# A two-layer graph network on one core: node products moved in layer 0's drain, and mixes one chunk further ahead in layer 1's tables

## The chip, the cores and the metric

The kernel runs on one core of a Trainium2 chip (trn2). Its time is device time in microseconds (us). The core's engines are TensorE (PE in the profile; PEld is its weight loading), VectorE (DVE), ScalarE (ACT), GpSimd (POOL) and SyncE (SP, which issues most of the transfers). Each engine takes its own queue of instructions, and engines wait for each other through semaphores.

## What is computed

The reference runs two message-passing layers on a graph of 6250 nodes with 128 features and 106250 edges, sorted by destination (100000 random ones and a loop at each node). Cut to what matters:

```python
h = relu(layernorm(x))
# layer 0: attention (GATv2) with a residual, gelu, batch norm over nodes
m = leaky_relu(xl[src] + xr[dst] + edge_attr @ We, 0.2)      # xl = h @ Wl + bl, xr = h @ Wr + br
logits = m @ att
alpha = softmax of logits over the edges of one dst
h0 = gelu(h + segment_sum(xl[src] * alpha, dst) + bias_out)
x = x + ((h0 - mean) * rsqrt(var + eps) * bn_gamma + bn_beta) # mean, var over all nodes
# layer 1: messages, gate and update
h = relu(layernorm(x))
em = relu(layernorm(concat(h[src], h[dst]) @ msg_w + msg_b)) * edge_weight
messages = segment_mean(em, dst)
h_new = relu(layernorm(concat(h, messages) @ upd_w + upd_b))
x = x + gate * h_new + (1 - gate) * h                         # gate = sigmoid(h @ gate_w + gate_b)
```

## The kernel before, in words

The program holds two arms and a flag that the data decide; the sorted input takes the arm `fast()`, and only it is spoken of here. `fast()` works under a manual schedule: on each engine the instructions stand in the order in which the Python code issues them, and waits come from the data.

The edges are cut into NS = 99 blocks of up to 8 tiles of 128 edges (the last has 5 tiles). The loops of a node's own go into the per-node steps. The nodes are 49 tiles of 128, in NGR = 13 groups (`GS`): eleven of 4 tiles (groups 0 to 10), one of 3 (group 11) and one of 2 (group 12).

**Layer 0** is a loop over rounds `s` (line 1407), 0 to 106. Round s gathers block s from the table xl_d (POOL, L187), expands the destination rows by one-hot matmuls (L1132) and makes the logits. Every SB = 4 blocks a generator `maxima` takes the segment maxima over the tiles of four blocks (the last one of three): a transpose on PE (L1181), scans on DVE (L1184 to L1189), transposes of the ends (L1192, L1193), a row of carries on DVE (`crow`, L1196 to L1204), its transposes (L1208), a second scan (L1211 to L1215), an exp on ACT (L1216), and transposes back (L1219, L1220) to the factors `exm` (L1224). LAG = 7 rounds later, block u = s - 7 is weighted by these factors (`glw`: L1439 and L1444 on DVE, L1446 on ACT), summed by 8 one-hot matmuls in `agg_ps` (L1483, of two passes each in the profile), copied by ACT (L1321, in `flush` one round later) and stored to one of two tables by block parity (L1135, SP). After round 98 only this second half runs: this is the drain. In it DVE and ACT each make half of a block's weights.

The node groups run behind: `due` (from `rounds_of(LAG)`, L1153) names the round in which group g begins, and each later round takes one step of its generator `nodes(g)` (L1232). Its first step fetches the two result tables (`fetch`, L1141) and xl, and makes the products of the tile's own loop, `up`: for each tile one matmul with a single row (`ones` by `blr`, L1246) and one with the group's columns of h (`wlr`, L1247). Two empty steps follow. Then come the loop's logit and the maximum (L1253 to L1268) and an exp (L1269), then the factors (L1272 to L1276), the scaling of the three parts (in the last three groups partly on ACT, L1280, with L1282 and L1284 on DVE) and the transposes (L1295), then the sum into h and the gelu (L1297, L1299), then the batch-norm statistics (L1303). Before, group 10 is due in round 98 and group 11 in round 104. Group 12 begins after the loop: its steps and those left of group 11 are interleaved by `in_turn(group, nodes(NGR - 1), "baabbbabbab")` (L1504), where each letter takes one step of group 11 (a) or 12 (b).

**Layer 1's tables** (from L1527) first turn the batch-norm statistics to a scale A and shift B, and then go through 13 chunks of 4 node tiles. For chunk c: `mix(c)` on DVE adds the scaled h to x (L1548), `centre(c)` on PE takes off the mean (L1553), `split(c)` on ACT makes the squares and the relu (L1559, L1560) and on POOL shifts x (L1561). PE then makes the variance (`var_ps`, L1584) and the product with the message and gate weights (`mm`, L1589), ACT the root (L1593), DVE its reciprocal (L1594) and the table rows (L1598), which SP stores to a_d (L1603). In the rounds of chunks 1 to 3 the first part of the destination table b_d is made beside this, by the generator `part_rows`: one DVE operation per round (L1003, then L1007 twice), each followed by a cast on ACT (L1005, L1005, L1008). In round c, before, `mix(c + 2)` stands at the start.

**Layer 1** is a second loop over the 99 blocks, which gathers from a_d (L187) and ends with the output. The change doesn't touch it.

Of the kernel before, what the change touches and what calls it, by code (L numbers as in the profile page):

```python
# [9 lines left out]
F32 = mybir.dt.float32  # L10
# [7 lines left out]
P = 128  # L18
D = 128
# [12 lines left out]
ST = 8  # L32
# [20 lines left out]
TN = 4  # L53
# [13 lines left out]
def kernel(  # L67
# [855 lines left out]
    def fast():  # L923
# [235 lines left out]
        with tc.tile_pool(name="e0", bufs=2) as ep, tc.tile_pool(  # L1159
# [16 lines left out]
            def maxima(b):  # L1176
# [52 lines left out]
                yield  # L1229
                yield  # L1230

            def nodes(g):  # L1232

                t0, n = G0[g], GS[g]
                ns = slice(t0 * P, (t0 + n) * P)
                last = g == NGR - 1
                fin = np_.tile([P, 2, n if last else TN, WF], F32, name="fin", tag="tab_p" if last else "fin")
                xl = np_.tile([P, n if last else TN, WL], F32, name="xl", tag="tab_x" if last else "xl")
                fetch(fin, res0_d, t0, n)
                nc.sync.dma_start(xl[:, :n, :], xl_d[t0 * P : (t0 + n) * P].rearrange("(t p) f -> p t f", p=P))  # L1240
                if last:
                    up = ps_m.tile([P, ST, D], F32, name="m_ps")[:, :n, :]
                else:
                    up = ps_1.tile([P, TN, D], F32, name="up", tag="np")[:, :n, :]
                for j in range(n):
                    T.matmul(up[:, j, :], ones[0:1, :], blr[0:1, :], start=True, stop=False)  # L1246
                    T.matmul(up[:, j, :], h_sb[:, t0 + j, :], wlr, start=False, stop=True)  # L1247
                yield
                yield
                yield  # L1250

                ea, lo = (small.tile([P, TN], F32, name=f"own_l{k}")[:, :n] for k in range(2))
                V.tensor_add(ea, fin[:, 0, :, D + 2][:, :n], fin[:, 1, :, D + 2][:, :n])  # L1253
                for j in range(n):
                    V.scalar_tensor_tensor(up[:, j, :], We_r, ea[:, j : j + 1], up[:, j, :],
                                           op0=ALU.mult, op1=ALU.add)
                V.scalar_tensor_tensor(up, up, 0.0, over_tiles(att8, n), op0=ALU.max, op1=ALU.mult)
                V.tensor_reduce(lo, up, AX.X, ALU.add)
                V.scalar_tensor_tensor(lo, ea, wa, lo, op0=ALU.mult, op1=ALU.add)
                top, den = fin[:, :, :n, D], fin[:, :, :n, D + 1]  # L1260
                mm = small.tile([P, 3, TN], F32, name="mm0")[:, :, :n]
                V.tensor_scalar(mm[:, :2, :], den, 0.0, -BIG, op0=ALU.is_equal, op1=ALU.mult)
                V.tensor_add(mm[:, :2, :], mm[:, :2, :], top)
                V.tensor_add(mm[:, 2, :], lo, xl[:, :n, D])
                mx = small.tile([P, TN], F32, name="mx0")[:, :n]
                V.tensor_tensor(mx, mm[:, 0, :], mm[:, 1, :], ALU.max)
                V.tensor_tensor(mx, mx, mm[:, 2, :], ALU.max)
                V.tensor_tensor(mm, mm, mx[:, None, :].to_broadcast([P, 3, n]), ALU.subtract)  # L1268
                S.activation(mm, mm, AF.Exp)  # L1269
                yield  # L1270
                dd = small.tile([P, 2, TN], F32, name="dd")[:, :, :n]
                V.tensor_mul(dd, den, mm[:, :2, :])  # L1272
                V.scalar_tensor_tensor(dd[:, 0, :], dd[:, 0, :], 1e-16, dd[:, 1, :], op0=ALU.add, op1=ALU.add)
                V.tensor_add(dd[:, 0, :], dd[:, 0, :], mm[:, 2, :])
                V.reciprocal(dd[:, 0, :], dd[:, 0, :])
                V.tensor_tensor(mm, mm, dd[:, 0:1, :].to_broadcast([P, 3, n]), ALU.mult)  # L1276
                if g >= NGR - 3:
                    for j in range(n):
                        for o, k in ((fin[:, 1, j, :D], 1), (xl[:, j, :D], 2)):
                            S.activation(o, o, AF.Copy, scale=mm[:, k, j : j + 1])  # L1280
                    for j in range(n):
                        V.scalar_tensor_tensor(fin[:, 0, j, :D], fin[:, 0, j, :D], mm[:, 0, j : j + 1],  # L1282
                                               fin[:, 1, j, :D], op0=ALU.mult, op1=ALU.add)
                    V.tensor_tensor(fin[:, 0, :n, :D], fin[:, 0, :n, :D], xl[:, :n, :D], ALU.add)  # L1284
                for j in range(n if g < NGR - 3 else 0):
                    V.tensor_scalar(fin[:, 0, j, :D], fin[:, 0, j, :D], mm[:, 0, j : j + 1], None, op0=ALU.mult)
                    for o, k in ((fin[:, 1, j, :D], 1), (xl[:, j, :D], 2)):
                        V.scalar_tensor_tensor(fin[:, 0, j, :D], o, mm[:, k, j : j + 1],
                                               fin[:, 0, j, :D], op0=ALU.mult, op1=ALU.add)
                if last:  # L1290
                    tp = ps_m.tile([P, ST, D], F32, name="m_ps").rearrange("p j f -> p (j f)")
                else:
                    tp = ps_1.tile([P, CH], F32, name="np")
                for j in range(n):
                    T.transpose(tp[:, j * P : (j + 1) * P], fin[:, 0, j, :D], ident)  # L1295
                yield
                V.scalar_tensor_tensor(hT_sb[:, ns], tp[:, : n * P], bias_c, hT_sb[:, ns],  # L1297
                                       op0=ALU.add, op1=ALU.add)
                S.activation(hT_sb[:, ns], hT_sb[:, ns], AF.Gelu)  # L1299
                if last:  # L1300
                    S.activation(std_c[:, 0:1], eps, AF.Sqrt)
                yield
                V.bn_stats(bns[:, g, :], hT_sb[:, t0 * P : min((t0 + n) * P, N)])  # L1303
# [98 lines left out]
            due = rounds_of(LAG)  # L1402
            turns = {r + 6: g for r, g in due.items() if g < NCH - 3}
            turns.update({3: NCH - 3, 8: NCH - 2, 13: NCH - 1})
            begun = breaks()
            spread(0)
            for s in range(NS + LAG + 1):
# [76 lines left out]
                if s < NS:  # L1484
                    if s % SB == SB - 1:
                        steps = maxima(s // SB)
                    next(steps, None)
                if s < 5:
                    zero(res0_d, WF, 2 * s)
                    zero(res0_d, WF, 2 * s + 1)  # L1490
# [32 lines left out]
        with tc.tile_pool(name="md", bufs=3) as mp, tc.tile_pool(  # L1523
# [22 lines left out]
            def mix(c):  # L1546
                cs, n = chunk(c)
                V.scalar_tensor_tensor(xT_sb[:, cs], hT_sb[:, cs], A, xT_sb[:, cs], op0=ALU.mult, op1=ALU.add)  # L1548
# [22 lines left out]
            centre(0)  # L1571
            mix(1)
            split(0)
            for c in range(NC):
                cs, n = chunk(c)
                ts = slice(c * TN, c * TN + n)
                if c + 2 < NC:
                    mix(c + 2)
                if c + 1 < NC:
                    centre(c + 1)  # L1580
                var = ps_v.tile([P, TN], F32, name="var_ps")
                sq = sqs.pop(c)
                for j in range(n):
                    T.matmul(var[:, j : j + 1], sq[:, j * P : (j + 1) * P], avg, start=True, stop=True)  # L1584
                outs = []
                for j in range(n):
                    t = c * TN + j
                    mm = ps_t.tile([P, D + 1], F32, name="mm")
                    T.matmul(mm, hT_sb[:, t * P : (t + 1) * P], wm, start=True, stop=True)  # L1589
                    outs.append(mm)  # L1590
                if c + 1 < NC:
                    split(c + 1)
                S.activation(std_c[:, ts], var[:, :n], AF.Sqrt, bias=eps)  # L1593
                V.reciprocal(rstd_c[:, ts], std_c[:, ts])  # L1594
                tab = mp.tile([P, TN, D + 1], F32, name="tab")
                for j, mm in enumerate(outs):
                    r = rstd_c[:, c * TN + j : c * TN + j + 1]
                    V.scalar_tensor_tensor(tab[:, j, :], mm, r, b1[:, : D + 1], op0=ALU.mult, op1=ALU.add)  # L1598
                tabs[c] = tab
                if c:  # L1600
                    gates(c - 1)
                rows_ = slice(c * CH, c * CH + n * P)
                nc.sync.dma_start(a_d[rows_].rearrange("(t p) f -> p t f", p=P), tab[:, :n, :D])  # L1603
                if c == 1:
                    bp = ps_b.tile([P, TN, D], F32, name="b_ps")
                    b_product(bp, 0)
                    made = b_rows(mp, bp, 0)
                if made is not None:
                    next(made, None)
# [328 lines left out]
```

## Time and profile before

| | us |
|---|---|
| median of 3 runs | 2219.21 (2216.82 to 2223.94) |
| the profiled execution | 2221.45 |
| its span, first to last instruction | 2219.7 |
| layer 0's rounds with gathers, about | 80 to 1075 |
| drain of layer 0, about | 1075 to 1128 |
| layer 1's tables, about | 1128 to 1173 |
| layer 1's blocks, about | 1173 to the end |

| stretch | PE busy | DVE busy | ACT busy | POOL busy | granted PE clock |
|---|---|---|---|---|---|
| 1075 to 1128 (53 us) | 30.4 | 37.2 | 25.3 | 0.0 | 0.73 |
| 1128 to 1173 (45 us) | 40.2 | 28.5 | 23.0 | 20.2 | 0.89 |
| 1173 to 2219 (1046 us) | 511.7 | 789.0 | 784.1 | 754.5 | 0.66 |

A row of the profile names the engine, the line, the operation and what it writes and reads; a number in brackets is the idle time of the engine just before, with what ended it. `x16` stands for 16 instructions merged in one row. The granted clock is what the throttle gave TensorE as a share of full speed: it is 0.50 or 1.00 at any time, and values between are means over a stretch.

### The profile page before, as it was taken

The page shows a single profiled execution, that of the slowest core. Times are in us where ns is not written, and L with a number is a line of the kernel's source. Part 1 is how long each engine was busy: PE and PEld are TensorE (multiplying, and loading weights), DVE is VectorE, ACT ScalarE, POOL GpSimd, SP SyncE. Part 2 cuts the span into 40 slices and gives each one's busy share as a digit, 9 for nine tenths or more (in the row PEclk, how much of TensorE's full clock was granted, in tenths as well). Part 3 has the DMA queues.
Part 4 walks back from the last instruction along what each step waited for, and adds up shares of the span by engine and source line. Part 5 has one row for each costly group of instructions (what it writes and reads, how often), then busy time and mean ns, then how long its engine had stood idle before and what let it go on. Part 6 is the DMA issues. An engine that isn't in the chain of part 4 may idle for free. (4 is left out here: it accounts for less than half of the span.)

```text
span 2219.7 us, 28197 instructions
## 1 busy us (share of the span) xinstructions
PE 1144.3 (52%) x6261; PEld 1020.3 (46%) x6261; DVE 1688.3 (76%) x3887; ACT 1288.3 (58%) x4330; POOL 1564.0 (70%) x1630
## 2 busy tenths in 40 slices
PE   5224555655655654645763455554554554554554
PEld 3124444544544544544652344554544554544443
DVE  8668887787787787787764677787787787887786
ACT  6224344443543444443445777777787787777785
POOL 4677777777777777777236777777777777777770
PEclk9556666566665666566776666666666666666666
DMA  5664456444435534534223343443443444343441
GB/s 143 179 181 108 108 141 179 114 95 117 111 88 115 117 82 116 120 84 108 59 61 100 89 109 93 107 109 93 107 111 95 103 114 104 92 114 93 102 112 39
DMA packets 243537, 239.21 MB, mean 108 GB/s; under 512 B 90720, under 2 KB 186921, under 8 KB 243359
## 3 DMA queue, kind: packets, MB, share of 16 engines
q0 software_dynamic: 50496, 103.92, 21.9%
q1 hardware_dynamic: 192575, 133.27, 21.6%
q8 instruction: 52, 0.85, 0.2%
q14 instruction: 126, 1.03, 0.2%
q10 hardware_dynamic: 288, 0.13, 0.0%
HBM read 189.20 MB, written 47.96 MB: 107 GB/s over the span
## 5 line engine op out<-in xcount | busy, mean ns | idle before, releaser
L187 POOL DMA_INDIRECT gl<-xl_d,src_c x789 | 766.3, 971 | 267.5 <-issue 169.7
L187 POOL DMA_INDIRECT gl<-a_d,src_c x789 | 754.5, 956 | 246.3 <-issue 178.3
L1483 PE MATMUL agg_ps<-glw,oh 128*128 128x131 f32 x1536 | 338.4, 407 | 218.7 <-ACT agg L1321 160.0
L1483 PEld LDWEIGHTS agg_ps<-glw,oh 128*128 128x128 f32 x1536 | 314.8, 310 | 239.0 <-ACT agg L1321 221.7
L1865 PE MATMUL agg_ps<-glw,oh 128*128 128x130 f32 x1040 | 235.4, 414 | 328.6 <-ACT glw L1853 320.6
L1865 PEld LDWEIGHTS agg_ps<-glw,oh 128*128 128x128 f32 x1040 | 217.8, 312 | 341.7 <-ACT glw L1853 341.7
L1831 ACT ACTIVATE sq<-y 128x128 f32<-128x128 f32 x789 | 243.8, 309 | 108.4 <-DVE y L1823 86.6
L1446 ACT ACTIVATE glw<-gl,exm 128x128 f32<-128x128 f32 x763 | 233.1, 388 | 0.0
L1452 ACT ACTIVATE m_ps<-m_ps 128x1024 f32<-128x1024 f32 (+1 forms) x99 | 99.5, 1005 | 216.2 <-DVE cc L1211 111.0
L1844 DVE SCALAR_TENSOR_TENSOR y<-y,rs,cst 128x128 f32<-128x128 f32 x789 | 211.6, 340 | 0.0
L1451 DVE TENSOR_TENSOR m_ps<-m_ps,gl 128x1024 f32<-128x1024 f32 (+1 forms) x99 | 121.6, 1229 | 117.4 <-DMA gl<-xl_d,src_c 102.9
L1865 PE MATMUL agg_ps<-ea_r,oh 128*128 128x130 f32 x512 | 117.9, 420 | 169.9 <-ACT ea_r L1853 161.5
L1132 PEld LDWEIGHTS <-oht 128*128 128x128 bf16 (+1 forms) x1578 | 144.0, 125 | 122.5 <-issue 52.0
L1865 PEld LDWEIGHTS agg_ps<-ea_r,oh 128*128 128x128 f32 x512 | 108.9, 318 | 176.2 <-ACT ea_r L1853 176.2
L1030 DVE TENSOR_SCALAR oht<-oht,third 120x1024 bf16<-120x1024 bf16 x198 | 100.1, 506 | 101.8 <-DMA oht<-dl_d 101.7
L1853 ACT ACTIVATE glw<-y,ew_c 128x128 f32<-128x128 f32 x528 | 161.5, 388 | 0.0
L1461 DVE TENSOR_TENSOR m_ps<-m_ps,att 128x1024 f32<-128x1024 f32 (+1 forms) x99 | 120.8, 1220 | 36.5 <-ACT m_ps L1452 35.6
L1831 ACT ACTIVATION_READ_ACCUMULATOR sq<-y 128x1 f32 x789 | 146.9, 186 | 0.0
L1823 DVE TENSOR_TENSOR y<-y_ps,gl 128x1024 f32<-128x1024 f32 (+1 forms) x99 | 119.5, 1207 | 33.9 <-PE agg_ps L1865 18.2
L1132 PE MATMUL m_ps<-W,oht 128*128 128x128 bf16 x789 | 88.8, 281 | 99.9 <-DVE lr L1463 94.9
L1849 ACT ACTIVATE y<-y 128x1024 f32<-128x1024 f32 (+1 forms) x99 | 104.3, 1054 | 36.3 <-DVE y L1846 36.3
L1463 DVE TENSOR_REDUCE lr<-m_ps 128x8 f32<-128x1024 f32 (+1 forms) x99 | 120.8, 1220 | 3.4
(348 smaller groups left out, 2227.5 us busy)
## 6 DMA issues: line engine op xcount, KB each, us to landing
oht<-dl_d SPq DMA_DIRECT2D x198, 240.0 KB
gl<-xl_d,src_c POOLq DMA_INDIRECT x789
gl<-a_d,src_c POOLq DMA_INDIRECT x789
res<-zt SPq DMA_DIRECT2D x20, 327.5 KB
res<-zt SPq DMA_DIRECT2D x20, 325.0 KB
res<-agg SPq DMA_DIRECT2D x99, 64.5 KB
res<-agg SPq DMA_DIRECT2D x99, 64.0 KB
W<-xr_d SPq DMA_DIRECT2D x198, 30.0 KB
```

The source lines that it names most:

```text
L187: return GP.indirect_dma_start(out=dest, out_offset=None, in_=table, in_offset=bass.IndirectOffsetOnAxis(ap=idx, axis=0))
L1132: T.matmul(ps[:, j, :], oht[:rows_, j * P : (j + 1) * P], w[:rows_, j // TN, :], start=True, stop=True)
L1446: S.activation(glw[:, j, :D], glu[:, j, :D], AF.Copy, scale=f)
L1451: passed[s] = [V.tensor_tensor(ps, ps, gl[:, :n, :D], ALU.add)]
L1461: passed[s].append(V.tensor_tensor(ps, ps, over_tiles(att8, n), ALU.mult))
L1463: V.tensor_reduce(lr, ps, AX.X, ALU.add)
L1483: T.matmul(aggs[u], oh[:, j, :], glw[:, j, :], start=(j == 0), stop=(j == m - 1))
L1823: added = V.tensor_tensor(y[:, :n, :], pss.pop(s)[:, :n, :], gl[:, :n, :], ALU.add)
L1831: S.activation(sq, y[:, j, :], AF.Square, accum_out=rs[:, j : j + 1])
L1844: marks.append(V.scalar_tensor_tensor(yu[:, j, :], yu[:, j, :], ru[:, j : j + 1], mg_ps, op0=ALU.mult, op1=ALU.mult))
L1853: S.activation(glw[:, j, :D], yu[:, j, :], AF.Copy, scale=ew_c[:, u, j : j + 1])
L1865: T.matmul(aggs[u], oh[:, j, :], glw[:, j, :], start=(j == 0), stop=(j == m - 1))
```

## The change

In layer 0 the products `up` get a function of their own, `lift(g, up)`. For groups 11 and 12 it is called in rounds 100 and 101, behind the sums of blocks 93 and 94, and writes to the two PSUM buffers `m_ps` of the expansion, which has none to write from round 99 on. Group 10 is due in round 99 instead of 98, so its fetch and its products stand at the end of that round. Groups 10 to 12 lose the third empty step. The last two groups get a new step boundary between ACT's scaling (L1280) and DVE's sums (L1282). The string of `in_turn` stays. In layer 1's tables, `mix(2)` moves ahead of the loop, and in round c `mix(c + 3)` stands behind the table rows (L1598) instead of `mix(c + 2)` at the start.

```diff
+            ups = {}
+
+            def lift(g, up):
+
+                t0, n = G0[g], GS[g]
+                ups[g] = up[:, :n, :]
+                for j in range(n):
+                    T.matmul(up[:, j, :], ones[0:1, :], blr[0:1, :], start=True, stop=False)
+                    T.matmul(up[:, j, :], h_sb[:, t0 + j, :], wlr, start=False, stop=True)
+
             def nodes(g):
...
-                if last:
-                    up = ps_m.tile([P, ST, D], F32, name="m_ps")[:, :n, :]
-                else:
-                    up = ps_1.tile([P, TN, D], F32, name="up", tag="np")[:, :n, :]
-                for j in range(n):
-                    T.matmul(up[:, j, :], ones[0:1, :], blr[0:1, :], start=True, stop=False)
-                    T.matmul(up[:, j, :], h_sb[:, t0 + j, :], wlr, start=False, stop=True)
-                yield
-                yield
-                yield
+                if g not in ups:
+                    lift(g, ps_1.tile([P, TN, D], F32, name="up", tag="np"))
+                up = ups.pop(g)
+                yield
+                yield
+                if g < NGR - 3:
+                    yield
...
                             S.activation(o, o, AF.Copy, scale=mm[:, k, j : j + 1])
+                    if g >= NGR - 2:
+                        yield
                     for j in range(n):
                         V.scalar_tensor_tensor(fin[:, 0, j, :D], fin[:, 0, j, :D], mm[:, 0, j : j + 1],
...
             turns.update({3: NCH - 3, 8: NCH - 2, 13: NCH - 1})
+            if NS - 1 in due:
+                due[NS] = due.pop(NS - 1)
...
                     next(steps, None)
+                elif s - NS in (1, 2):
+                    lift(NGR - 3 + s - NS, ps_m.tile([P, ST, D], F32, name="m_ps"))
...
             split(0)
+            mix(2)
             for c in range(NC):
                 cs, n = chunk(c)
                 ts = slice(c * TN, c * TN + n)
-                if c + 2 < NC:
-                    mix(c + 2)
...
                 tabs[c] = tab
+                if c + 3 < NC:
+                    mix(c + 3)
                 if c:
                     gates(c - 1)
```

## The prediction

> **What bounds the kernel now.** I read the page first, for the chain that ended last.
>
> ```profile
> DVE 19%; DMA 7%; ACT 6%; PE 5%; issue 5%; POOL 5%; DVEq 0%; SPq 0%; ACTq 0%; POOLq 0%
> ```
>
> These shares add up to 47% of the span. The chain of waits in order of time begins at 1170.17 us, with the last table product of layer 1, so it covers layer 1 alone. Both edits lie ahead of it: layer 0's drain (about 1075 to 1128 us) and layer 1's tables (1128 to 1173). POOL does no gather between 1071 and 1173.5, and layer 1's first gather is at 1173.56, so every microsecond won or lost there moves the whole of layer 1. Both places are chains of latency, so I read the timeline, first around the step that the change moves. Columns: start, duration, engine, line, operation, and in brackets the idle time before it and what ended it.
>
> ```profile
> 1079.71 0.75 PE L1247 MATMUL up<-wlr,h_sb 128*128 128x128 f32 x2
> 1080.26 0.42 PE L1181 MATMUL mx<-ident,lgc 128*21 128x128 f32 x1
> 1080.72 0.28 DVE L1184 COPY lt<-mx 21x128 f32<-21x128 f32 x1 [0.79 <-PE mx L1181]
> ...
> 1081.93 3.86 PE L1483 MATMUL agg_ps<-glw,oh 128*128 128x131 f32 x16
> ...
> 1085.72 0.23 PE L1208 MATMUL tx<-ident,crow 1*21 1x1 f32 x2
> 1085.99 0.15 DVE L1211 COPY cc<-tx 21x2 f32<-21x2 f32 x1 [1.47 <-PE tx L1208]
> ...
> 1088.37 0.19 DVE L1224 TENSOR_TENSOR exm<-tx,fst_c 128x21 f32<-128x21 f32 x1 [0.72 <-PE tx L1220]
> ```
>
> Two things show. Group 10's products (8 matmuls, 16 passes, from 1076.77) hold back the transpose L1181, and DVE waits 0.79 for it. And L1208 starts only when the 16 passes of block 92 end, though its input crow was done by 1082.5: PE's queue is what it waits for. After L1224 DVE is busy almost without a break to 1104.6 (its only gaps are 0.2 to 0.5 us behind ACT's scaling of group 10), and then waits for group 11's data:
>
> ```profile
> 1109.87 0.16 DVE L1253 TENSOR_TENSOR own_l<-fin 128x3 f32<-128x3 f32 x1 [5.28 <-DMA fin<-res]
> ...
> 1122.88 0.35 DVE L1282 SCALAR_TENSOR_TENSOR fin<-fin,mm 128x128 f32<-128x128 f32 x1 [1.01 <-ACT fin L1280]
> ```
>
> That fetch waits for block 96's store, hence for ACT's copy at 1104.48, which stands behind group 10's gelu, which stands behind DVE: 5.1 us of store and fetch that move with DVE, not slack. In the tables, chunks 1 to 3 take 4.0 us each and later ones 2.65 (PE's sums). This is one of the slow rounds, in the timelines of DVE and of ACT:
>
> ```profile
> 1146.66 1.13 DVE L1598 SCALAR_TENSOR_TENSOR tab<-mm,rstd_c,b 128x129 f32<-128x129 f32 x4
> 1147.70 0.69 DVE L1007 TENSOR_TENSOR tab_x<-tab_x,tab_p 128x512 f32<-128x512 f32 x1
> 1148.30 0.75 DVE L1548 SCALAR_TENSOR_TENSOR x_sb<-h_sb,bn,x_sb 128x512 f32<-128x512 f32 x1
> 1150.39 0.18 DVE L1594 RECIPROCAL rstd_c<-std_c 128x4 f32<-128x4 f32 x1 [1.34 <-ACT std_c L1593]
> ```
> ```profile
> 1148.42 0.62 ACT L1008 CAST tab_p<-tab_x 128x512 bf16<-128x512 f32 x1 [1.98 <-DVE tab_x L1007]
> 1148.95 0.68 ACT L1559 ACTIVATE sq<-ctr,bn 128x512 f32<-128x512 f32 x1
> 1149.53 0.68 ACT L1560 ACTIVATE h_sb<-ctr,bn 128x512 f32<-128x512 f32 x1
> 1150.10 0.26 ACT L1593 ACTIVATE std_c<-var_ps,eps 128x4 f32<-128x4 f32 x1
> ```
>
> The ring is L1593, L1594, L1598, L1007, cast, two split operations, L1593: 1146.09 to 1150.10. The mix L1548 lies outside it: it runs while DVE would wait 1.34 for L1593 anyway.
>
> **The change, part by part.** The order of instructions says what moves. DVE, ACT, PE and SP change only at the places below; POOL's queue is unchanged.
>
> (1) Group 10's products go behind block 92's sums on PE, ahead of L1208. In front, DVE finishes block 92's weights at 1079.93 and can take L1184 then: -0.79. Behind, L1208 waits for eight more matmuls. Their price depends on PE's clock, and the trace has both. In the drain they ran at full clock (0.415 us each, 3.3 in all). At half clock, PE's timeline has them 0.725 apart:
>
> ```profile
> 747.68 0.80 PE L1247 MATMUL up<-wlr,h_sb 128*128 128x128 f32 x2
> 748.40 0.79 PE L1246 MATMUL up<-blr,ones 1*128 1x128 f32 x2
> 749.12 0.80 PE L1247 MATMUL up<-wlr,h_sb 128*128 128x128 f32 x2
> ```
>
> Eight of them are 5.8 us. The Trainium skill (TensorE: Matmul & The Clock Gate, Part 1: The HAM clock gate) says that about 3.4 us of sustained PE work releases the clock. Block 92 and the products now stand back to back for at least 7 us, so by the rule the products would be at full speed: 3.3, and the step costs 3.3 - 0.8 = +2.5. The rows speak against it. The stretch table of the granted clock has 1.00 at 1077 to 1079 while only these products ran, then 0.90 and 0.50 from 1080; a group at 919.7 to 925.4 stays at 0.50 throughout though PE never rests. These products hardly count as activity. I take 5.8 - 0.8 = **+5.0**; low end +2.5.
>
> (2) Group 11's six products go between blocks 93 and 94 on PE, group 12's four between 94 and 95. Who waits: ACT's copy of block 94, and behind it in ACT's queue group 10's scaling (L1280, 1097.70); then group 10's transposes (L1295, 1101.10), behind block 95 on PE. Slack: block 94 ended at 1095.02 and could end at about 1097.4; block 95 ended at 1098.47, 2.6 ahead of the transposes. At full clock six products are 2.5, less PE's 0.40 wait there, and four are 1.7, less its 1.38 wait: 2.1 and 2.4 late, both hidden. At half clock they are 4.35 and 2.9, and blocks 94 and 95 lose 1.4 and 1.8 themselves: block 95 ends 3.95 + 1.4 + 1.5 + 1.8 = 8.6 late, 6.0 over the slack. So 0 to +6.0. Before, the clock came up at 1093.4, only after sums back to back; products now stand between those. I take a third, **+2.0**.
>
> (3) What those products leave: block 98's sums no longer wait for group 11's products (1106.78 to 1109.18). Its store must still wait until the fetch of group 11 has read the same table (stores 97 and 98 are issued from 1109.90), and group 12's first DVE step has no wait ahead of it: **0**.
>
> (4) Group 10's fetch moves past the store of block 91 on SP's queue (issued 1079.66) and waits for it, by block 96's example 1.75 us after the copy, then 3.4 to arrive: about 1085, against use at 1090.46. Its first step is 5.4 us later than that, so **0**; stores 92 and on are copied from 1085.8, when SP is free. The dropped third yield leaves its arithmetic in the same round.
>
> (5) In the last two groups, the extra yield lets group 12's four scalings (L1280) pass group 11's gelu and its table load, and on DVE L1272 to L1276 pass L1297. Before, the first scaling was at 1122.46, behind 1.28 + 0.45 us of gelu; now it starts when L1276 is done, about 1121.8, and the load runs under the transposes. L1284 ends 0.65 earlier: **-0.65** (0 to -1.0).
>
> (6) Mixes. DVE's order changes in three rounds only: where the b-table step (L1003, L1007, L1007) followed the table product directly, the mix now stands between. Three mixes from 1129.36 take 2.07, about 0.66 from start to start. That goes into the ring three times: 3 x 0.66 = **+2.0**. At most 3 x 1.11 (a mix beside POOL, 1157.85) = 3.3. PE's waits for mixes (0.27 at 1145.10, 0.64 at 1149.11) go, but what is late next is L1593, already the end of the ring. In the later nine rounds no DVE instruction stands between old and new place: 0.
>
> Sum: 5.0 + 2.0 - 0.65 + 2.0 = +8.35. The profiled execution took 2221.45 (span 2219.7, 1.75 around it), so it would be 2229.8; it lies 2.24 above the median 2219.21, which goes to **2227.6**.
>
> **Rivals.** Differences within 0.3% (6.7 us) count as no change.
>
> *The gate stays open in the drain.* Step 1 costs 2.5, step 2 nothing: 2.5 - 0.65 + 2.0 = +3.9, 2223.1. For it: the skill's rule, and full clock for six of the ten earlier groups of products. Against it: the drain has no expansion matmuls beside the sums. Chance 0.25.
>
> *Half clock all through.* 5.0 + 6.0 - 0.65 + 2.0 = +12.4, and up to 1.3 more for mixes beside POOL: 2231.6 to 2233. For it: 0.50 from 1080 to 1093. Against: a block of 3.86 us can fill a clock window by itself. Chance 0.13.
>
> *Not slower: PE decides in the tables.* PE's clock drops to 0.50 from 1151.5 to 1154.9, just behind its two waits for mixes; the products and centring there took 1.95 and 1.91 instead of 1.14 and 1.02. If earlier mixes keep PE fed, the waits (0.9) and the drop (1.7) go, so -2.6 in place of +2.0; it decides if ctr L1553 is what arrives last in chunks 3 to 5. With the first rival's drain that is 2.5 - 0.65 - 2.6 = -0.75, 2218.5. Against it: the ring closes at 4.0 us without PE. Chance 0.10.
>
> *It does nothing there:* both orders differ in the built program, so I give this none.
>
> **How the numbers follow.** The forecast, step 1 at half clock with step 2 between, has 0.52; its own range is +5.5 to +11, 2224.7 to 2230.2. The range reaches to the gate-open case (its low side, 2219.5) and to the half-clock one (2233.5). Slower by over 0.3%: most of the forecast (0.43) and the half-clock case (0.13), 0.56. Within: 0.41. Faster by over 0.3%: 0.03, as no cover found is worth 6.7 us.
>
> **What would show it.** Right: L1208 directly behind the products, 3 to 6 us later after L1193 than now; L1184 with no wait; L1224 later; the 5.28 wait at L1253 unchanged; L1282 of group 12 without its 1.01; L1593 to L1593 of 4.7 instead of 4.0 in chunks 1 to 3. Wrong: products at 0.415 behind block 92; a smaller wait at L1253, which would mean that the store was not tied to DVE; a ring that stays at 4.0.

## The result, and the profile after

| | before | changed |
|---|---|---|
| median, 20 runs each | 2218.0 us (2214.7 to 2223.9) | 2224.4 us (2216.9 to 2231.3) |
| ratio, 95% interval | | 1.0028 [1.0020, 1.0035] |
| the profiled execution, its span | 2221.45, 2219.7 | 2228.96, 2227.2 |

The changed kernel is slower by 6.4 us in the medians and by 7.5 us in the profiled pair. The chain line of the page of the changed kernel has the same shares as before, within two points:

```profile
DVE 17%; DMA 7%; ACT 6%; POOL 6%; issue 5%; PE 5%; DVEq 0%; SPq 0%; ACTq 0%; POOLq 0%
```

So the page doesn't tell where 7.5 us went; the timeline around the moved steps does. Line numbers are now those of the changed kernel: the products are L1239 and L1240 (before L1246, L1247), group steps L1260 and L1291 (before L1253, L1282), block sums L1494 (L1483), and in the tables the root L1605, its reciprocal L1606, the table rows L1610 and the mix L1561 (before L1593, L1594, L1598, L1548). Columns as in the prediction: start, duration, engine, line, operation, and in brackets the idle time before it with what ended it. First the drain, PE and DVE:

```profile
1081.89 3.86 PE L1494 MATMUL agg_ps<-glw,oh 128*128 128x131 f32 x16
1085.68 0.79 PE L1239 MATMUL up<-blr,ones 1*128 1x128 f32 x2
...
1090.74 0.80 PE L1240 MATMUL up<-wlr,h_sb 128*128 128x128 f32 x2
1091.47 0.23 PE L1208 MATMUL tx<-ident,crow 1*21 1x1 f32 x2
...
1091.73 0.15 DVE L1211 COPY cc<-tx 21x2 f32<-21x2 f32 x1 [7.26 <-PE tx L1208]
...
1094.12 0.19 DVE L1224 TENSOR_TENSOR exm<-tx,fst_c 128x21 f32<-128x21 f32 x1 [0.72 <-PE tx L1220]
...
1115.67 0.16 DVE L1260 TENSOR_TENSOR own_l<-fin 128x3 f32<-128x3 f32 x1 [5.32 <-DMA fin<-res]
...
1127.84 0.35 DVE L1291 SCALAR_TENSOR_TENSOR fin<-fin,mm 128x128 f32<-128x128 f32 x1
```

The transpose L1181 no longer has products ahead of it, and L1184 (1080.68) has lost its wait of 0.79. The eight products stand behind block 92 at half clock, 1085.68 to 1091.47 = 5.8 us; L1208 comes directly behind them, and DVE waits 7.26 instead of 1.47. The wait for group 11's fetch is 5.32 where it was 5.28: the delay passes through whole. Group 12's L1291 has no wait where it had 1.01. In the tables, a round of DVE and of ACT:

```profile
1152.76 1.13 DVE L1610 SCALAR_TENSOR_TENSOR tab<-mm,rstd_c,b 128x129 f32<-128x129 f32 x4
1153.80 0.74 DVE L1561 SCALAR_TENSOR_TENSOR x_sb<-h_sb,bn,x_sb 128x512 f32<-128x512 f32 x1
1154.46 0.68 DVE L1007 TENSOR_TENSOR tab_x<-tab_x,tab_p 128x512 f32<-128x512 f32 x1
1157.15 0.18 DVE L1606 RECIPROCAL rstd_c<-std_c 128x4 f32<-128x4 f32 x1 [2.01 <-ACT std_c L1605]
```
```profile
1155.18 0.62 ACT L1008 CAST tab_p<-tab_x 128x512 bf16<-128x512 f32 x1 [2.64 <-DVE tab_x L1007]
...
1156.86 0.26 ACT L1605 ACTIVATE std_c<-var_ps,eps 128x4 f32<-128x4 f32 x1
```

The mix stands inside the ring, 0.66 from start to start; DVE's wait at its end has grown from 1.34 to 2.01, and so has ACT's for the b-table step, 1.98 to 2.64. From root to root it is 4.67 where it was 4.01. But this is not all of the tables' loss. The stretch table of the changed kernel (stretch, its length, PE busy and rows, granted clock, share of the transfer engines, GB/s) goes on:

```profile
1156.00:1158.00 2.00, 0.83 (x8) 1.00 0.58 197
1158.00:1160.00 2.00, 1.96 (x12) 0.87 0.23 72
1160.00:1162.00 2.00, 2.00 (x8) 0.50 0.46 137
...
1166.00:1168.00 2.00, 2.00 (x18) 0.93 0.42 123
```

Behind the ring the clock is at 0.50 for 6.8 us (1159.5 to 1166.3). Before, it was there for 3.4 (1151.5 to 1154.9):

```profile
1150.00:1152.00 2.00, 1.81 (x13) 0.87 0.58 195
1152.00:1154.00 2.00, 2.00 (x8) 0.50 0.42 131
1154.00:1156.00 2.00, 2.00 (x13) 0.78 0.44 131
```

The two rounds there take 4.45 and 4.85 us instead of 4.73 and 2.65. In a later kernel with the mixes in their old place, whose clock stayed at 1.00 here (group 10 alone), they take 3.38 and 2.64.

The path from layer 0's last blocks to the last table row can be cut into five stages, by the starts of DVE's steps. They are the yardstick of all that follows (profiled executions, us):

| kernel | factors of the last full group of blocks to the last factors (L1224 to L1224) | to group 11's first step (L1260) | to the batch-norm sums | to the first mix | to the last table row | sum |
|---|---|---|---|---|---|---|
| before | 10.62 | 21.50 | 16.66 | 2.83 | 40.91 | 92.52 |
| changed | 15.53 | 21.55 | 15.83 | 2.82 | 44.66 | 100.39 |
| drain alone | 12.97 | 21.45 | 15.81 | 2.82 | 40.80 | 93.85 |
| mixes alone | 12.61 | 21.60 | 16.66 | 2.83 | 44.22 | 97.92 |
| drain alone, group 10 back | 11.04 | 21.45 | 15.82 | 2.82 | 41.58 | 92.71 |
| changed, full-row bias | 11.80 | 22.36 | 15.81 | 2.83 | 45.73 | 98.53 |
| before, cast late | 12.71 | 21.53 | 16.66 | 2.83 | 36.49 | 90.22 |
| changed, cast late | 15.53 | 21.43 | 15.83 | 2.82 | 36.29 | 91.90 |
| step boundary alone | 11.41 | 22.31 | 15.97 | 2.82 | 41.80 | 94.31 |
| boundary, full-row bias, cast late | 8.64 | 22.31 | 15.96 | 2.83 | 39.14 | 88.88 |
| changed, one extra product a round | 15.53 | 21.58 | 15.82 | 2.83 | 44.76 | 100.52 |
| changed, two extra products | 13.29 | 23.94 | 15.83 | 2.82 | 44.34 | 100.22 |
| group 10 alone | 13.05 | 21.43 | 16.65 | 2.82 | 39.21 | 93.16 |
| groups 11 and 12 alone | 10.84 | 21.38 | 16.51 | 2.82 | 39.11 | 90.66 |

Of the pair's 7.5 us, +4.9 lie in the first stage, -0.8 in the third and +3.75 in the last: 7.87 in all. Outside the stages 0.4 net comes back: they begin 0.8 later, and what follows them is 1.2 shorter.

### The profile page after: what moved, and what is told of

Read it like the earlier page. It is cut to its first block, busy times and chain, and to the rows that moved or that the text cites. A ratio compares the mean times of both kernels' runs of the same rounds, so it can differ in the third digit from the quotient of the medians.

```text
span 2227.2 us, 28194 instructions
## 1 busy us (share of the span) xinstructions
PE 1138.8 (51%) x6261; PEld 1013.4 (46%) x6261; DVE 1688.5 (76%) x3887; ACT 1288.5 (58%) x4330; POOL 1561.2 (70%) x1630
## 3 DMA queue, kind: packets, MB, share of 16 engines
q1 hardware_dynamic: 192575, 133.27, 21.6%
## 5 line engine op out<-in xcount | busy, mean ns | idle before, releaser
L1494 PE MATMUL agg_ps<-glw,oh 128*128 128x131 f32 x1536 | 330.6, 400 | 214.4 <-ACT agg L1330 163.3
L1494 PEld LDWEIGHTS agg_ps<-glw,oh 128*128 128x128 f32 x1536 | 307.6, 303 | 234.4 <-ACT agg L1330 218.5
L1879 PEld LDWEIGHTS agg_ps<-glw,oh 128*128 128x128 f32 x1040 | 216.8, 311 | 345.8 <-ACT glw L1867 345.8
```

The costliest lines, as they stand in the source:

```text
L1494: T.matmul(aggs[u], oh[:, j, :], glw[:, j, :], start=(j == 0), stop=(j == m - 1))
L1879: T.matmul(aggs[u], oh[:, j, :], glw[:, j, :], start=(j == 0), stop=(j == m - 1))
```

## The experiments

The theory was the prediction's mechanism: group 10's products hold up L1208, the mixes lengthen the ring, the rest costs little. Its rivals stand with each run. All medians are beside those of the kernel before on the same chip; only the ratios are compared between runs. An "about" figure in us is the measured ratio times the median of before. The ratio need not be the quotient of the two medians shown (with group 10 alone it is 1.0014, the quotient 1.0009), and its interval reaches 1.7 to 2.5 us to each side.

**The two halves.** The changed kernel with the mixes put back, and the kernel before with only the mixes moved (the diff is of the first; the second has the same lines the other way round):

```diff
-            mix(2)
...
+                if c + 2 < NC:
+                    mix(c + 2)
...
-                if c + 3 < NC:
-                    mix(c + 3)
```

> The drain's edits alone, the mixes at their old place. Queue theory: L1208 waits behind group 10's eight products at half clock, so L1224 to the first mix is as in the changed kernel; +4.1 us against before (4.9 for the products, 0.8 back from the step boundary), and the rounds of chunks 1 to 3 take 4.0 us again. Clock rival (what costs is that PE's clock is at half speed for longer in drain and tables, whatever the order): the tables lose as much as in the changed kernel, 3.7 us, and the sum stays near +7.

Measured: 2215.97 against 2214.17, ratio 1.0011 [1.0000, 1.0021], about +2.4 us. Here the clock came up to 1.00 under block 92's sums, the products took 0.415 each, and DVE waited less for L1208:

```profile
1086.63 0.15 DVE L1211 COPY cc<-tx 21x2 f32<-21x2 f32 x1 [4.72 <-PE tx L1208]
```

> The mixes one chunk ahead alone, the drain as before. Ring theory: rounds of chunks 1 to 3 take 4.67 instead of 4.0 us, +2.0 against before, and up to 1.7 more if the half-clock stretch behind them is one clock window longer. Rival (PE decides in the tables and gains from earlier mixes): rounds stay at 4.0 or less, PE's waits of 0.27 and 0.64 go, -0.9 to -2.6.

Measured: 2217.39, 1.0019 [1.0012, 1.0027], about +4.2 us; rounds of 4.68, 4.68, 4.66 in place of 4.0, and behind them 4.61 and 4.66, so the last stage is 44.22. The halves make 1.0011 + 0.0019 = 1.0030, the whole 1.0028. In this run's unchanged drain the products, in front, ran at half clock, and the first stage took 12.61 where before it was 10.62. So two executions of one order differ by 2 us there, two fifths of what the pair shows for the step: the pair of before and changed is no fair pair for it.

**Group 10 back.** The drain alone, with group 10 due in round 98 again (its third step kept):

```diff
-                if g < NGR - 3:
+                if g < NGR - 2:
                     yield
...
-            if NS - 1 in due:
-                due[NS] = due.pop(NS - 1)
```

> Drain edits alone, but group 10 due in round 98 as before: its fetch and its products stand ahead of L1181 again, while groups 11 and 12 keep their early products and the step boundary. Queue theory: L1208 starts behind block 92 as in before, DVE waits 1.5 instead of 7.3 us for it; what is left is -0.8 from the boundary and the products between blocks 93, 94 and 95, 0 where the clock is up and up to +6 where it is not: -0.8 to +2. Rival (the lifted products of groups 11 and 12 are what costs): +4, as with group 10 moved.

Measured: 2216.82, 1.0012 [1.0003, 1.0020]. Its profile says that the first stage's loss is gone (11.04), but its median is as slow as that of the whole drain. This disagreement was taken up again below.

**Full rows for the bias.** The changed kernel, with the one-row product of `ones` and `blr` replaced by one of the identity and all 128 rows of `blr`, which are alike; the count and the places stay:

```diff
-                    T.matmul(up[:, j, :], ones[0:1, :], blr[0:1, :], start=True, stop=False)
+                    T.matmul(up[:, j, :], ident, blr, start=True, stop=False)
```

> The changed kernel with one edit: the bias product of a group uses the identity and all 128 rows of the bias instead of one row of ones and one of the bias; same result, same number of matmuls. If a one-row product counts little for the clock and the pairs are slow because of the mix of one row and 128 rows, the eight products of group 10 take less than 5.8 us (3.9 at half clock if a pass then takes the 0.24 us of a block's sums, less if the clock rises under them), L1208 comes 2 to 3.5 us earlier and the kernel is 2 to 4 us faster than the changed one. If the rows don't matter: 5.8 us again, no change.

Measured: 2218.60, 1.0024 [1.0014, 1.0033], not told apart from the changed kernel: the 2 to 4 us expected can't be seen. But the products behave quite differently, PE's timeline:

```profile
1084.43 0.64 PE L1239 MATMUL up<-blr,ident 128*128 128x128 f32 x2
1084.86 0.56 PE L1240 MATMUL up<-wlr,h_sb 128*128 128x128 f32 x2
1085.26 0.39 PE L1239 MATMUL up<-blr,ident 128*128 128x128 f32 x2
```

They start 0.43 apart at half clock and 0.22 apart at full clock, where the mixed ones take 0.725 and 0.415. The clock comes up at 1085.2, while they run; that it did so because of them is not shown here, as the last 3.4 us before it held 2.8 us of block 92's sums. The first stage fell from 15.53 to 11.80; the tables of this execution took 45.73 and its first table round 2 us more, and the median kept little of it.

**The cast late.** In both kernels, the b-table step with its cast is issued behind the root instead of at the end of the round before, so that ACT's cast no longer stands ahead of the splits; this takes the ring apart.

```diff
                 S.activation(std_c[:, ts], var[:, :n], AF.Sqrt, bias=eps)
+                if made is not None:
+                    next(made, None)
...
-                if made is not None:
-                    next(made, None)
             gates(NC - 1)
```

> The kernel before with one edit in the tables: the b-table step of a round (one DVE operation and its cast on ACT) is issued behind the next chunk's root L1593 instead of at the end of the round, so that the cast no longer stands ahead of the split. Ring theory: rounds of chunks 1 to 3 fall from 4.0 to about 2.7 us, -3.9, and the half-clock stretch behind them goes or shrinks (-0.8): -4 to -5 in all. Rival (PE or DVE's own load sets the 4.0): no change in the rounds.

Measured: 2211.22 against 2214.65, 0.9984 [0.9977, 0.9992], 3.5 us faster than before. Root to root is 3.60 once and otherwise 2.64 or 2.65, and ACT's rows show why: the cast now stands behind the root, waits 0.45 there for DVE, and no split or root of its own chunk waits behind it.

```profile
1144.66 0.26 ACT L1593 ACTIVATE std_c<-var_ps,eps 128x4 f32<-128x4 f32 x1
1145.37 0.62 ACT L1005 CAST tab_p<-tab_x 128x512 bf16<-128x512 f32 x1 [0.45 <-DVE tab_x L1007]
```

> The changed kernel with the same edit, so mixes one chunk ahead and the cast off the ring. If the mixes cost only through the ring, the tables take as long as in the kernel before with that edit (about 36 us from the first mix to the last table row), and what is left against before is the drain's +1.5 to +4 less the ring's 4 to 5: -3 to 0. If the earlier mixes cost by themselves (beside POOL, or in front of the reciprocal), the tables stay 2 us longer than there.

Measured: 2213.27, 0.9997 [0.9985, 1.0008]. The tables take 36.29, as with the mixes in the old place (36.49). So the mixes' place costs nothing of itself; it costs because it stands in a ring that closes last. With the ring gone PE was busy without a break through the rounds that follow, and the clock stayed at 1.00, in both kernels.

**The step boundary alone, and the best of the parts.** First the kernel before with only step 5 of the prediction; then this with the full-row bias and the late cast:

```diff
-                yield
+                if g < NGR - 2:
+                    yield
...
+                    if g >= NGR - 2:
+                        yield
```

> The kernel before with the step boundary of the last two groups alone (and the third empty step of those two dropped); no products moved, mixes as before. Queue theory: from group 11's first step to the batch-norm aggregate 15.8 instead of 16.7 us, and nothing else moves: -0.8, at the edge of what the runs can tell. If the gain in the changed kernel came from the early products of groups 11 and 12 instead: no gain here.

Measured: 2212.97 against 2214.65, 0.9994 [0.9985, 1.0002]: about -1.3 us, the interval just reaching no change. The third stage is 15.97 for 16.66.

> What the runs point to: the kernel before with the step boundary (-0.8), the cast off the ring (-4 to -5), and the bias product over all 128 rows, which at 0.22 to 0.43 us a matmul makes group 10's products ahead of L1181 short enough that DVE no longer waits for L1181 (-0.8, more where the clock is at half). Sum -5.5 to -8 against before. If the products stay 0.4 to 0.7 each in that place: -5 at most.

Measured: 2208.85, 0.9978 [0.9969, 0.9988], 4.9 us faster than the kernel before, a little short of the 5.5 expected. The cast alone gave 3.5 and the boundary alone 1.3, so no gain from the full rows can be told; the intervals of this kernel and of the late cast alone (0.9977 to 0.9992) overlap.

**Is it idle time that brings the clock down behind the ring?** The changed kernel with work added that nothing reads: one 128x512 product in each of rounds 2 to 4.

```diff
+                if 2 <= c <= 4:
+                    more = ps_b.tile([P, TN, D], F32, name="b_ps")
+                    T.matmul(more.rearrange("p t f -> p (t f)"), cen, hT_sb[:, cs], start=True, stop=True)
```

> The changed kernel with work added: in rounds 2 to 4 of the tables PE makes one more 128x512 product into a PSUM bank that nothing reads (0.9 us a round at full clock, inside a round of 4.67). Theory: what the tables lose beyond the ring's 2.0 us comes from PE's idle time in the long rounds, which lets the clock fall to half just behind them. Then the clock stays at 1.00 through the tables, the rounds behind the ring fall from 4.45 and 4.85 to about 2.7, and from the first mix to the last table row it is 41 us instead of 44.7, against before about +3 in all. Rival (those rounds are long for another reason, such as the table rows or POOL): they stay, and the added products make it no shorter than 44.7.

Measured: 2219.68 against 2215.01, 1.0016 [1.0007, 1.0025], and a miss: the clock still fell, from 1156.5 to 1163.3, and the two rounds took 4.62 and 4.74. PE still had waits, though (the stretches from 1152 to 1156 have 1.46 and 1.66 busy of 2.00). So a second product went behind the centring of rounds 3 to 5:

```diff
+                if 3 <= c <= 5:
+                    more = ps_b.tile([P, TN, D], F32, name="b_ps")
+                    T.matmul(more.rearrange("p t f -> p (t f)"), cen, xT_sb[:, slice((c + 1) * CH, (c + 2) * CH)], start=True, stop=True)
```

> The changed kernel with two extra products in each table round instead of one: the 128x512 product behind the variances of rounds 2 to 4, as in the run before, and another of the same size behind the centring of the chunk after, for three rounds, so that TensorE's wait for the standard deviation is filled too. Nothing reads them; they are work added. Theory (the clock falls behind the long rounds because TensorE idles in them): granted clock 1.00 from 1135 to 1170 us, the two rounds behind the ring 2.7 us instead of 4.5 and 4.85, the tables from the first mix to the last row about 41 us instead of 44.7. Rival (the clock falls for another reason, or the two rounds are long for another reason): the clock falls to 0.50 there as in the changed kernel and the tables stay at 44.7 us. If the clock stays at 1.00 and the tables still take 44 us, the half clock is not what lengthens those rounds.

Measured: 2218.41 against 2214.35, 1.0018 [1.0007, 1.0029]. The clock held, in the stretch table of this kernel:

```profile
1140.00:1142.00 2.00, 2.00 (x14) 0.83 0.49 139
...
1156.00:1158.00 2.00, 2.00 (x13) 1.00 0.46 154
1158.00:1160.00 2.00, 2.00 (x15) 1.00 0.42 131
```

PE is busy throughout, and the rounds behind the ring take 3.07 and 2.65 instead of 4.45 and 4.85, though the ring itself is at 4.68, 4.68, 4.66. That part of the theory holds: if PE never rests in the ring, the clock stays and these rounds are short. The expected 41 us for the tables was missed all the same (44.34): here the clock came up only at 1140.7, 3.6 us behind the first root where it was 1.1 us ahead of it in the changed kernel, and the first round took 4.73 instead of 2.75; and the round in which the ring ends, with an extra product in it, took 2.33 instead of 1.40. The drain of this execution gave something more, told below.

**The drain's steps one by one.** The profiles gave the loss to step 1; the medians of the kernel with group 10 back (1.0012) and of the one with the boundary alone (0.9994) gave it to step 2. So each was put alone into the kernel before: group 10's move (`due` and its third step), and the `lift` calls in rounds 100 and 101.

> The kernel before with one thing of the change: group 10's products behind the sums of block 92, ahead of the transposes of the weights (its third yield dropped, so that its arithmetic stays in its round). The products of groups 11 and 12, the step boundary and the mixes are as before. Theory by the traces (step 1 carries the drain's loss, the products of groups 11 and 12 cost nothing): about +2.5 us against before, a ratio of 1.0011, DVE waiting 4.7 us (full clock) or 7.3 us (half clock) for the transposes. Rival by the medians (the kernel with group 10 back in its place was as slow, 1.0012, as the one with the whole drain, 1.0011; so step 1 costs nothing in most executions): a ratio of 0.9995 to 1.0003.

Measured: 2215.99 against 2214.11, 1.0014 [1.0004, 1.0024], about +3.1 us; its products ran at 0.415 and DVE waited 4.79. The traces' theory holds, and the rival by the medians falls, narrowly (its highest ratio is 1.0003).

> The kernel before with one thing of the change: the products of groups 11 and 12 between blocks 93, 94 and 95, in banks of their own. Group 10, the step boundary and the mixes are as before. Theory by the traces (these products are hidden: the stage from the weights' last step to group 11's first has 21.5 us in the changed kernel and before): a ratio of 0.9997 to 1.0003 and that stage 21.5 us, or 22.4 us at half clock. Rival by the medians (group 10 back, 1.0012, against the step boundary alone, 0.9994): these products cost about +4 us in the middle of the executions, a ratio of 1.0018, and where the profiled execution shows it, blocks 94 and 95 end later and that stage takes 24 to 27 us.

Measured: 2213.30, 1.0001 [0.9990, 1.0013], the second stage 21.38. So the products of groups 11 and 12 are hidden in the middle of the executions, as far as 2.5 us can be told.

## Why the prediction was right, and where its sizes were off

The time came out 3.2 us below the 2227.6 forecast, inside its range and on the side that it named; +6.4 us is 0.29%, so it lies just inside the bound of 0.3%, with an interval to both sides; the prediction had thought it a little more likely to lie outside. The mechanism was right in each place: L1208 behind the products, the wait at L1260 unchanged, the ring longer by one mix. The sizes, step by step:

| step of the prediction | forecast | this pair's profiles | alone, by the ratios |
|---|---|---|---|
| 1, group 10's products ahead of L1208 | +5.0 | +4.9 | +3.1 |
| 2, products of groups 11 and 12 | +2.0 (0 to 6) | 0 | +0.2 |
| 5, step boundary | -0.65 | -0.8 | -1.3 |
| 6, mixes in the ring | +2.0 | +3.75 | +4.2 |
| sum | +8.35 | +7.85 | +6.2 |

The sum is better than its terms, and that is luck: step 2 was put about 2 us too high and step 6 about 2 us too low, and the two errors cancel. That the last column comes so near the 6.4 measured proves little either, as each of its terms is known to about 2 us.

**Step 1 mixed two clocks.** It set the products' half-clock price behind block 92 (5.8) against the 0.8 that they cost in front, as L1184's wait, at full clock. But in front they have a half-clock price too: with the old order the first stage took 10.6 to 11.0 where they ran mostly at full clock (before, group 10 back, groups 11 and 12 alone; 11.4 in the boundary alone) and 12.6 to 12.7 where they ran at half (mixes alone, before with the late cast). There DVE's wait for L1181, 0.79 in the trace of before, is longer, here with the mixes alone:

```profile
1081.48 0.28 DVE L1184 COPY lt<-mx 21x128 f32<-21x128 f32 x1 [2.95 <-PE mx L1181]
```

With the new order it took 13.0 to 13.3 at full clock (drain alone, group 10 alone, two extra products) and 15.53 at half (changed, its late cast, one extra product). Like for like that is +2.3 at full and +2.9 at half clock, and +4.9 only across. The profiled execution of before happened to be fast there and that of the changed kernel slow. The prediction read the first from one execution and took it for the kernel.

The rule that was weighed there, of the Trainium skill (TensorE: Matmul & The Clock Gate, Part 1: The HAM clock gate), that about 3.4 us of sustained work releases the clock, was neither refuted nor right for the products. Changes of the clock in one trace are always a multiple of 3.413 us apart (in the trace of before 1076.38, 1079.80, 1093.44). These stretches of 3.413 us, called windows here, lie otherwise in each execution. Where a window is filled by a block's sums it ends at 1.00: with group 10 alone, block 92 ran from 1078.36, and the window from 1078.8 ended at 1082.2 with full clock, just as the products began. In the changed kernel the block began at 1081.89, 0.9 us into a window, so no window was full of sums; and from then to 1091.7 PE never rested, nearly three windows, and the clock stayed at 0.50.

All fourteen traces together show more. From the last expansion product to group 11's first step they have 88 windows at half clock, and the time that PE spent on block sums in a window sorts them: those with 2.67 us or less were followed by 0.50, those with 2.72 or more by 1.00. Pairs of a one-row and a 128-row product made no difference to this: a window with 2.59 of sums that they filled to the end was followed by 0.50, and so were those that they filled alone. One window breaks the order, and it is the one with most full-row products, 1.97 us of them and 1.16 of sums in the best of the parts, followed by 1.00. Nor did the pairs hold the clock: five traces have a window at full clock with 2.9 to 3.4 us of pairs and under 0.5 of sums, and each was followed by 0.50. This order was found in the traces; no edit was made to test it. So the prediction's reading "these products hardly count as activity" was right, and "at half clock" was right for half of the six profiled executions that have this order with the one-row bias. The first rival, with the gate open, is what the other half did.

**Step 2 was a mean over cases, and the usual case is 0.** The second stage is 21.4 to 21.6 with these products between the blocks (changed, drain alone, groups 11 and 12 alone) and without (before, mixes alone, group 10 alone). The chain that the prediction described does exist; one of the profiled executions, that with two extra products in the tables, showed it by chance, since nothing in its drain differs from the changed kernel:

```profile
1096.21 3.67 PE L1494 MATMUL agg_ps<-glw,oh 128*128 128x131 f32 x16
...
1099.97 0.27 ACT L1330 COPY agg<-agg_ps 128x131 f32<-128x131 f32 x1 [3.81 <-issue]
...
1100.57 0.35 DVE L1291 SCALAR_TENSOR_TENSOR fin<-fin,mm 128x128 f32<-128x128 f32 x1 [2.94 <-ACT fin L1287]
```

Group 11's products run at half clock, block 94's sums end at 1099.9, ACT's copy (here L1330) waits 3.81, and DVE waits 2.94 for the scaling behind that copy; the stage takes 23.94, 2.4 more. In the changed kernel the clock came up at 1098.0, under the first of them, and the copy waited 0.40. So +2.4 is a case, not the rule. The stages of 22.3 and 22.4 (full-row bias, boundary alone, best of the parts) occur with and without these products, and are not theirs; in each of the three the clock fell for one window under a later block, which took 3.4 to 3.7 us instead of 2.0 to 2.1.

**Steps 3 and 4** cost 0 as said: no wait stands in the trace at group 10's or 12's first step. **Step 5** is -0.7 to -0.85 by the trace in every kernel that has it, within its range.

**Step 6 had the ring right and stopped there.** Three rounds went from 4.0 to 4.67, three times 0.66 = +2.0, as forecast. What it left out is what the longer ring does to PE: the long rounds leave PE waiting, the clock falls behind them, and in this pair does so for two windows instead of one (6.8 us for 3.4); the rounds behind the ring took 9.3 for 7.4, +1.9. Here too one execution stood for the kernel. With the mixes outside the ring the clock fell in two of six profiled executions (before, drain alone), for one window, and not at all in the other four, where these two rounds took 6.0. With the longer ring it fell for two windows in all four that did not keep PE busy throughout (changed, mixes alone, full-row bias, one extra product). So the mixes cost 2.0 + 1.9 or 2.0 + 3.3 us, by what the clock did behind the old ring; the +4.2 of the mixes alone lies between. The third rival had seen this place, but with the sign turned: it hoped that earlier mixes would feed PE and keep its clock. PE was not short of mixes; it waited for the ring.

The fall was stopped in two ways, by taking the ring apart (the late cast, in both kernels) and by filling PE (two extra products), so it is shown that in the tables PE's rest in the ring is what lets the clock fall, though for the filling by one profiled execution only. It lets the clock fall and doesn't force it, as the four executions above show. Why it lasts two windows and not one is not: PE was busy all through each of these windows in both kernels. Nor does PE's busy share of a window alone decide a fall: in the changed kernel a window with 0.56 was followed by 1.00, and one with 0.66 by 0.50; before, one with 0.76 was followed by 0.50. And the kernel with the drain alone but group 10 back (1.0012) is slower than its parts by themselves (1.0001 and 0.9994) make likely. With intervals this wide that can be chance; no profile shows a cause.

## What to carry to other kernels

Price a moved step on both sides at the same clock, and read the old place in more than one execution if the clock there can be either: the trace of before priced the old place at 0.8 us, and in other executions of the same order that stage was 2.0 longer. Of the place to which an instruction moves, ask not only whether its engine has time to spare there but whether the place lies between two links of a ring that closes last; where it does, take the ring apart first (moving the b-table step and its cast behind the root gave 3.5 us, and then the mix's place cost nothing). And where a longer round makes TensorE rest, add what its clock costs in the rounds after it, and look in several executions for how often it falls.

## What the runs showed of the hardware

Pairs of a one-row and a 128-row product of 128x128 f32 took 0.725 us a product at half clock and 0.415 at full; with 128 rows in both they took 0.43 and 0.22. So a product with a single row cost not less than a full one but made the pair dearer by 70 to 90%. In the drain the clock went from half to full behind windows with 2.72 us or more of block sums of 3.41; the mixed pairs did not count towards it, and 1.97 us of full-row products did in the one window that tells. The clock changed on a grid of 3.413 us, whose phase differs between executions; by the profiles, the first stage took 2.0 (old order) or 2.5 us (new order) more or less by the clock it met.
